# Row sums among the second heads, a projection one row tile later, and a scaling between two exponentials: three reorderings in a graph-attention and diffusion kernel

## The chip, the cores and the metric

The kernel runs on one NeuronCore of a Trainium2 chip. Its engines work side by side, each through its own queue of instructions: PE (TensorE, matrix products and transposes into the PSUM memory), DVE (VectorE), ACT (ScalarE), POOL (GpSimd), and SP (SyncE), which here only starts DMA transfers. The metric is the device time of one execution in microseconds (us), the median of several runs; lower is better.

## What is computed

N = 2708 nodes with 512 features, a dense adjacency `adj` of zeros and ones. Two layers follow one another. Both begin with a layer norm and a relu and add their result to their input. The first is graph attention with 8 heads of 64 features:

```python
feats  = einsum('nf,hfd->hnd', X, W)
dense  = e_self[:, :, None] + e_neigh[:, None, :]
dense  = where(dense >= 0, dense, 0.2 * dense) + NEG_INF * (1 - A)
out    = einsum('hnm,hmd->hnd', softmax(dense), feats) + b
```

The second diffuses features over two graphs, the given one and one that it builds itself from queries and keys, by keeping the most probable nine tenths of a softmax:

```python
S  = adj + eye(n)
Rf = S / S.sum(axis=1, keepdims=True)      # row sums
Rb = S / S.sum(axis=0)[:, None]            # column sums
for s in range(2):
    A  = nucleus(softmax(Xa @ W1 @ W2 @ (Xa @ W3).T), 0.9)
    Xf, Xb, Xa = Rf @ Xf, Rb @ Xb, A @ Xa
    Z += Xf @ U1[s] + Xb @ U2[s] + Xa @ U3[s]
```

A last layer norm of X + Z closes it. The sums of the rows of `adj` are used in the second layer, and in the first one for nodes that have no neighbour at all.

## The kernel before

The nodes are 22 row tiles (`NT`) of 128 rows, the last one of 20.

**Layer 0, the heads (L434-L499).** The columns are cut into four chunks of six row tiles (the last of four). For a chunk, `adj_t` is loaded for all 22 row tiles (`a_f`, L449), converted by ACT to `a_c` (L451), and stored with the unit matrix added as `s_d` (L456) for the second layer. Then come two groups of four heads, in the text the first heads and the second heads (`gi` = 0 and 1). For each row tile `t` DVE makes four tiles `e` of attention weights (L474), one a head, and PE multiplies each with the features into six accumulators `po` (L480). After the 22nd row tile ACT copies `po` to `o_t` (L487), and the next heads can start to fill them.

`row_sums(t)` (L337-L349) sums a row tile of `adj`: twice, a DMA on SP loads half of it into the one buffer `arow` (L345), ACT passes over it with a running sum (L346); then POOL makes three tiny results (L347-L349). In the program, the row sums of a chunk's own tiles stand right behind the chunk's loads, ahead of its heads.

The tiles of a finished chunk are completed during the first heads of the next chunk, by stages that `finished(t, ...)` returns (L359-L432). `later[slot]` holds the stages that run behind row tile `slot` (0 to 21 are the first heads, 22 to 43 the second), and a chunk's tile `i` puts its stages at

```python
later.setdefault(n if final else 3 * i + n + n // 4, []).append(stage)
```

so that a tile begins every three row tiles. The stages are `turned` (six transposes of `o_t` into the two PSUM tiles `pn0` and `pn1`, L372), `shared` (division by the softmax sums), `normed` (residual and layer norm, L401), `cleared` (ACT makes `v`, L416) and `asked`. This last one transposes `v` into `pn0` (L423), has ACT copy it to `v_t` (L425), splits `v` in two halves for later products (L426), and calls `project` (L171-L189): four products of `v_t` into `pn1` (L176), two ACT copies of it (L181, L182), three POOL operations (L186-L188) and a store of keys and queries to `kq_d` (L189). Of `pn0` and `pn1` there is one buffer each. Tiles of the last chunk are finished behind the loop and leave their projection to layer 1.

The heads do not stand under `manual_schedule`: for each engine the framework itself orders the instructions that are ready, and the order of the program is a preference between them. In layer 1, `manual_schedule` keeps PE, ACT, DVE and SP in the program's order.

**Layer 1, the start of step 0 (L1314-L1446).** The rows are taken in pairs (`G` = 2). For each pair, PE makes logits, DVE their maxima, ACT the exponentials: `exp()` returns steps, first two passes per tile, `root` and `full` (L601, L608), then `points` on POOL, then passes that count (`look`, L601). Beside it, PE multiplies `s_d` with the features (`part`, L1011-L1106), a list of steps called `others`; the last step of the second part is `scaled`, in which ACT scales the four PSUM results into `yo` (L1069); the next part needs these PSUM tiles. `late()`, called once with g = -1, runs

```python
paced(fills, 2 * G)
paced(others, 1)
others.extend(part(half, 2))
paced(others, NT // 2)
paced(fills, 2 + 3 * G * NA // 2)
```

where `paced(steps, n)` runs the first n steps: here `fills` are the steps of `exp()` of the second pair and `others` holds only `scaled`.

Of the kernel before, what the change touches and what calls it, by code (L numbers as in the profile page):

```python
# [54 lines left out]
def kernel(  # L55
# [26 lines left out]
    NT = -(-N // P)  # L82
# [9 lines left out]
    G = 2  # L92
# [78 lines left out]
    def project(pool, pk, v_t, t, s, bufs=None):  # L171


        pr = rows[t]
        for k in range(KD):
            nc.tensor.matmul(pk[:, :pr], lhsT=kw[:, k, :], rhs=v_t[:, k, :pr], start=(k == 0), stop=(k == KD - 1))  # L176
        big = pool.tile([P, P], F32, name="kq_b", bufs=bufs)
        hl = pool.tile([P, 2, P], F32, name="kq_hl", bufs=bufs)
        if pr < P:
            nc.gpsimd.memset(hl, 0.0)  # L180
        nc.scalar.copy(hl[:, 1, :pr], pk[:, :pr])  # L181
        nc.scalar.mul(big[:, :pr], pk[:, :pr], 4097.0)  # L182


        high, x = hl[:, 0, :pr], hl[:, 1, :pr]
        nc.gpsimd.tensor_tensor(high, big[:, :pr], x, op=OP.subtract)  # L186
        nc.gpsimd.tensor_tensor(high, big[:, :pr], high, op=OP.subtract)
        nc.gpsimd.tensor_tensor(x, x, high, op=OP.subtract)  # L188
        nc.gpsimd.dma_start(out=kq_d[s][:, :, t * P:(t + 1) * P], in_=hl)  # L189

    def split_rows(pool, eng, x, t, to):

        pr = rows[t]
        hl = pool.tile([P, 2, D], F32, name="split_hl")
        if pr < P:
            nc.gpsimd.memset(hl, 0.0)
        nc.vector.tensor_scalar(hl[:pr, 0].bitcast(I32), x.bitcast(I32), -4096, None, op0=OP.bitwise_and)
        eng.tensor_tensor(hl[:pr, 1], x, hl[:pr, 0], op=OP.subtract)
        nc.gpsimd.dma_start(out=to[t * P:(t + 1) * P], in_=hl)
# [19 lines left out]
    with ExitStack() as l0:  # L219
# [113 lines left out]
        halves = l0.enter_context(tc.tile_pool(name="l0halves", bufs=1))  # L333
# [25 lines left out]
        def finished(t, o_t, c0, bank, final):  # L359


            pr = rows[t]
            pns, held = [], []

            def turned():
                xt = work.tile([P, D], F32, name="xt0", bufs=4)
                nc.sync.dma_start(out=xt[:pr], in_=x[cols[t], :])
                held.append(xt)
                for g in range(NG):
                    pns.append(bank(g))  # L370
                    for k in range(len(beside)):
                        nc.tensor.transpose(pns[g][:pr, k * P:(k + 1) * P], o_t[:, g, k, c0:c0 + pr], ident)  # L372

            def shared():
                den = small.tile([P, H], F32, name="den")
                rden = small.tile([P, H], F32, name="rden")
                o = work.tile([P, D], F32, name="o", bufs=4)
                held.append(o)
                o3 = o.rearrange("p (h d) -> p h d", h=H)

                def halves(x, n):
                    return x[:, :2 * n].rearrange("p (i d) -> p i d", i=2)

                def turns(g):
                    return pns[g][:pr, :3 * P].rearrange("p (i d) -> p i d", i=2)

                for g in range(NG):
                    nc.vector.tensor_scalar(halves(den[:pr, g * HG:], 2), turns(g)[:, :, P::P // HG],
                                            lone_n[:pr, t:t + 1], None, op0=OP.add)
                nc.vector.reciprocal(rden[:pr], den[:pr])  # L390
                for g in range(NG):
                    c = slice(g * HG * DH, (g + 1) * HG * DH)
                    nc.vector.scalar_tensor_tensor(halves(o[:pr, c], 2 * DH), halves(fsum[:pr, c], 2 * DH),
                                                   lone[:pr, t:t + 1], turns(g)[:, :, :P], op0=OP.mult, op1=OP.add)
                eng = nc.vector if final else nc.gpsimd
                eng.tensor_mul(o3[:pr], o3[:pr], rden[:pr].unsqueeze(2).to_broadcast([pr, H, DH]))
                eng.tensor_add(o[:pr], o[:pr], b_b[:pr])

            def normed():
                xt, o = held  # L400
                nc.vector.scalar_tensor_tensor(o[:pr], o[:pr], 0.0, xt[:pr], op0=OP.max, op1=OP.add)  # L401
                held.extend(moments(small, o[:pr], pr))
                with_beta(o)

            def with_beta(o):
                xt = held[0]
                nc.gpsimd.tensor_add(xt[:pr], o[:pr], beta_b[:pr])
                nc.gpsimd.dma_start(out=xb_d[cols[t], :], in_=xt[:pr])

            def cleared():  # L410
                _, o, mean, rs = held
                v = turn.tile([P, D], F32, name="v")
                held.append(v)
                shift = small.tile([P, 1], F32, name="shift")
                nc.vector.scalar_tensor_tensor(shift[:pr], mean, -1.0, rs, op0=OP.mult, op1=OP.mult)
                nc.scalar.activation(v[:pr], o[:pr], AF.Relu, scale=rs, bias=shift[:pr])  # L416
                nc.gpsimd.dma_start(out=va_d[cols[t], :], in_=v[:pr])

            def asked():
                v = held[4]  # L420
                pt = bank(0).rearrange("p (k d) -> p k d", k=KD)
                for k in range(KD):
                    nc.tensor.transpose(pt[:, k, :pr], v[:pr, k * P:(k + 1) * P], ident[:pr, :pr])  # L423
                v_t = work.tile([P, KD, P], F32, name="v_t", bufs=2)
                nc.scalar.copy(v_t[:, :, :pr], pt[:, :, :pr])  # L425
                split_rows(halves, nc.gpsimd, v[:pr], t, vhl_d)  # L426
                project(halves, bank(1), v_t, t, 0, bufs=2)

            def rest():
                unasked.append((t, held[4]))  # L430

            return [turned, shared, normed, cleared, rest if final else asked]  # L432

        later = {}  # L434
        unasked = []
        for ci, tiles in enumerate(tchunks):
# [4 lines left out]
            for t in range(NT):  # L441
# [12 lines left out]
                    d = slice(t * P - n0, t * P - n0 + pr)  # L454
                    nc.gpsimd.tensor_tensor(a_f[:pr, d], a_f[:pr, d], ident[:pr, :pr], op=OP.add)
                nc.sync.dma_start(out=s_d[t * P:(t + 1) * P, n0:n0 + wide], in_=a_f[:, :wide])  # L456
            for t in tiles:
                row_sums(t)
            r_bs += [shares(grp, n0, cw) for grp in hgroups[1:]]
            o_t = work.tile([P, NG, len(beside), WC], F32, name="o_t", bufs=1)  # L460
            halfs = -(-cw // 512)
# [3 lines left out]
            for gi, (grp, r_b) in enumerate(zip(hgroups, r_bs)):  # L465
                po = [[ps_o.tile([P, 512], F32, name="po") for _ in parts] for _ in beside]
                for t in range(NT):
                    pr = rows[t]
                    es = []
                    for k, slots in enumerate(beside):  # L470
                        while len(es) <= max(i for i, _ in slots):
                            i = len(es)
# [16 lines left out]
            final = ci == len(tchunks) - 1  # L489
            for i, t in enumerate(tiles):  # L490
                if final and i < 3:
                    bank = lambda g: ps_o.tile([P, 512], F32, name="po")
# [486 lines left out]
    for s in range(STEPS):  # L979
        last = s == STEPS - 1  # L980
        with ExitStack() as st:
# [136 lines left out]
            def paced(steps, n):  # L1118
                for step in steps[:n]:
                    step()  # L1120
                del steps[:n]
# [171 lines left out]
            with tc.manual_schedule(engines={PE, ACT, DVE, SP}):  # L1293
# [52 lines left out]
                for g in range(-1, NP):  # L1346
# [48 lines left out]
                    def late(g=g):  # L1395
                        if g >= 0:
                            out_ = rest_of(att)
                            if last:
                                done.extend(zip(pairs[g], out_))
                            else:  # L1400
                                mixed(pairs[g], out_, others, fills, final)
                            keeps = 0
                            while last and keeps < len(others) and others[-1 - keeps].price == 0:
                                keeps += 1
                            while len(others) > keeps or fills:
                                if last:
                                    advanced(others, min(2, len(others) - keeps))
                                else:
                                    paced(others, 2)
                                paced(fills, 1)  # L1410
                            left.extend(others)
                            others.clear()
                            for t, y in done:
                                while t not in whole:
                                    paced(left, 1)
                                settled(t, y)
                            return


                        if last:  # L1420
                            paced(fills, len(fills))
                        else:
                            paced(fills, 2 * G)
                            paced(others, 1)
                            others.extend(part(half, 2))
                            paced(others, NT // 2)
                            paced(fills, 2 + 3 * G * NA // 2)
                            looks.extend(fills)
                        if last:
                            paced(others, len(others))  # L1430
# [51 lines left out]
```

## Time and profile before

| | us |
|---|---|
| median of 3 runs (lowest, highest) | 3473.28 (3465.6, 3474.12) |
| the profiled execution | 3485.01 |
| its span, first to last instruction | 3483.2 |
| layer 0, the heads | 139 to 943 |
| row sums, first and last load | 182.5 and 474.7 |
| ACT's waits for their loads | 165.8 in 42 waits |
| projections of finished tiles (L176) | 379.8 to 893.1, 18 tiles |
| start of step 0, the scaling `yo` | 1067.6 to 1070.0 |
| mean granted clock of PE | 0.964 |

A row of the timeline has the start, the length, engine, line, operation, output and inputs, and in brackets how long the engine stood idle before and what ended that. `x48` joins that many records; an fp32 product is two records on PE. A row of the waits has the waiting and the releasing instruction, the sum, the number and the longest wait in us. A row of the windows has the stretch, its length, each engine's busy time (with records), the clock granted to PE as a share of full speed, the share of the DMA engines that is busy, and GB/s.

### The profile page before, as it was taken

What the parts mean: (1) busy time and instruction counts of PE and PEld (TensorE: products, weight loads), DVE (VectorE), ACT (ScalarE), POOL (GpSimd) and SP (SyncE); (2) the same over time, 40 slices, a digit from 0 to 9 for tenths busy, and PEclk for the clock granted to TensorE, in tenths of its full rate; (3) what the DMA queues carried; (4) which work ended last, traced back from release to release, by engine and by line L of the source; (5) the groups of instructions that cost most, each with busy time, mean ns of one, the idle gap of its engine ahead of it and who ended that gap; (6) DMA issues with size and microseconds to landing.
All of it is one profiled execution on the core that took longest, in us unless ns stands there. A gap on an engine that the chain in (4) does not pass through costs nothing. (4 is left out here: it accounts for less than half of the span.)

```text
span 3483.2 us, 44354 instructions
## 1 busy us (share of the span) xinstructions
PE 3205.4 (92%) x16033; PEld 1707.6 (49%) x16033; DVE 2582.7 (74%) x4485; ACT 1501.5 (43%) x2219; POOL 923.6 (27%) x1091
## 2 busy tenths in 40 slices
PE   8988899899988999999999999899989999988898
PEld 4542333333455446455464643555555555555554
DVE  4577899888947655463655643887999899988984
ACT  2333231011036675564667521265644554455610
POOL 4212743605231221221222222110230232213211
PEclk9998999999999999999999998999999999999999
DMA  4478554222286336244452634766444554556453
GB/s 134 157 235 267 193 169 144 75 94 80 76 299 235 113 106 208 99 166 165 142 198 98 212 112 134 263 237 203 146 156 157 202 177 144 190 175 225 150 209 123
DMA packets 240046, 580.65 MB, mean 167 GB/s; under 512 B 32863, under 2 KB 66107, under 8 KB 239657
## 3 DMA queue, kind: packets, MB, share of 16 engines
q1 hardware_dynamic: 217721, 503.38, 43.3%
q0 software_dynamic: 22064, 74.09, 5.6%
q8 instruction: 127, 2.08, 0.2%
q14 instruction: 134, 1.10, 0.1%
HBM read 471.68 MB, written 105.68 MB: 166 GB/s over the span
## 5 line engine op out<-in xcount | busy, mean ns | idle before, releaser
L1165 PE MATMUL a<-va,at 128*128 128x512 f32 (+2 forms) x1936 | 887.8, 598 | 4.9 <-ACT at L1147 4.9
L480 PE MATMUL po<-e,fw 128*32 128x384 f32 (+3 forms) x7392 | 685.1, 507 | 58.5 <-DVE e L474 29.4
L474 DVE SCALAR_TENSOR_TENSOR e<-r_b,kk,a_c 128x768 f32<-128x768 f32 (+3 forms) x704 | 667.3, 1007 | 76.9 <-PE po L480 67.9
L601 ACT ACTIVATE junk_a<-p,nth 128x2708 uint8<-128x2708 f32 (+1 forms) x240 | 612.8, 2553 | 35.3 <-POOL nth L616 30.8
L1039 PE MATMUL q<-hl,s_r 128*128 128x512 f32 x1936 | 545.4, 430 | 66.4 <-DMA s_r<-s_d 46.0
L1165 PEld LDWEIGHTS a<-va,at 128*128 128x128 f32 (+2 forms) x1936 | 338.2, 186 | 374.6 <-issue 342.8
L1039 PEld LDWEIGHTS q<-hl,s_r 128*128 128x128 f32 x1936 | 370.1, 195 | 229.4 <-issue 68.2
L480 PEld LDWEIGHTS po<-e,fw 128*32 128x32 f32 (+1 forms) x7392 | 256.0, 112 | 451.5 <-issue 270.2
L1147 ACT COPY at<-t 128x512 f32<-128x512 f32 (+3 forms) x308 | 140.8, 478 | 647.1 <-PE t L1143 643.3
L680 DVE SCALAR_TENSOR_TENSOR junk<-p,th 128x2708 bf16<-128x2708 f32 (+1 forms) x132 | 409.5, 3102 | 3.0
L1059 PE MATMUL q<-u_k,v 128*128 128x512 f32 x704 | 318.2, 594 | 1.1 <-ACT v L1049 1.1
L1042 PE MATMUL q<-s_r,hl 128*128 128x512 f32 (+1 forms) x1056 | 283.2, 414 | 28.8 <-DMA s_r<-s_d 17.9
L1042 PEld LDWEIGHTS q<-s_r,hl 128*128 128x128 f32 x1056 | 196.8, 192 | 108.5 <-issue 54.1
L1059 PEld LDWEIGHTS q<-u_k,v 128*128 128x128 f32 x704 | 134.0, 191 | 159.8 <-issue 155.0
L569 ACT COPY p<-t 128x452 f32<-128x452 f32 (+2 forms) x264 | 130.9, 537 | 172.5 <-PE t L567 131.9
L876 DVE MAX8 vn<-keep 128x8 f32<-128x2708 f32 (+1 forms) x66 | 196.8, 2981 | 2.3
L567 PE MATMUL t<-keys,q_t 128*128 128x452 f32 x528 | 156.4, 420 | 40.1 <-ACT p L569 39.5
L594 DVE TENSOR_REDUCE nmx<-p 128x1 f32<-128x2708 f32 (+1 forms) x44 | 130.5, 2967 | 65.4 <-ACT p L569 65.4
L1212 PE MATMUL a<-u_k,v_t 128*128 128x512 f32 (+1 forms) x352 | 169.0, 619 | 5.5 <-ACT yo L1219 3.3
L155 POOL TENSOR_SCALAR ln_rs<-ln_mv 128x1 f32<-128x1 f32 x66 | 49.7, 754 | 407.9 <-DVE ln_mv L154 406.7
L1143 PEld LDWEIGHTS t<-ident,keep 128*128 128x128 f32 (+1 forms) x968 | 114.7, 139 | 77.0 <-issue 47.3
L1143 PE MATMUL t<-ident,keep 128*128 128x128 f32 (+1 forms) x968 | 145.2, 272 | 3.1 <-ACT p L569 3.0
(311 smaller groups left out, 3436.2 us busy)
## 6 DMA issues: line engine op xcount, KB each, us to landing
hl<-vhl_d SPq DMA_DIRECT2D x132, 512.0 KB
s_r<-s_d SPq DMA_DIRECT2D x264, 256.0 KB
hl<-fhl_d SPq DMA_DIRECT2D x132, 512.0 KB
hl<-bhl_d SPq DMA_DIRECT2D x132, 512.0 KB
u_k<-in_L_gnn_U_dram SPq DMA_DIRECT2D x184, 256.0 KB
arow<-in_adj_dram SPq DMA_DIRECT2D x42, 677.0 KB
s_d<-a_f SPq DMA_DIRECT2D x66, 384.0 KB
s_r<-s_d SPq DMA_DIRECT2D x132, 192.0 KB
```

Source lines behind the costliest of these rows:

```text
L474: nc.vector.scalar_tensor_tensor(es[i][:pr, :cw], r_b[:pr, i, :cw], kk[:pr, t, grp[i]:grp[i] + 1], a_c[t][:pr, :cw], op0=OP.max, op1=OP.mult)
L480: nc.tensor.matmul(po[k][n][q * w:(q + 1) * w, :b - a], lhsT=of if d < DH else of.to_broadcast([pr, w]), rhs=es[i][:pr, a:b], start=(t == ...
L567: nc.tensor.matmul(pl[:, :c1 - c0], lhsT=q[:, i], rhs=self.keys[:, c0:c1], start=(i == 0), stop=(i == 1))
L601: nc.scalar.activation(junk[:pr], self.p[i][:pr], func, **kw)
L680: nc.vector.scalar_tensor_tensor(self.junk_b[:pr], p, th, p, op0=OP.is_ge, op1=OP.mult, accum_out=dst)
L876: v.max(vs, keep[0][:pr])
L1039: nc.tensor.matmul(half[j], lhsT=s_r[:, j * P:(j + 1) * P], rhs=hl[:, h], start=(c == 0 and h == 0), stop=(c == NT - 1 and h == 1))
L1042: nc.tensor.matmul(half[j][:, :w], lhsT=hl[:, h, j * P:(j + 1) * P], rhs=s_r[:, :w], start=(c == 0 and h == 0), stop=(c == NT - 1 and h == 1))
L1059: nc.tensor.matmul(half[j], lhsT=across_t[-1][k][:, j * P:(j + 1) * P], rhs=u_k, start=(start and k == 0), stop=(start and k == KD - 1))
L1143: nc.tensor.transpose(pt[:rows[c], j, :pr], keep[i][:pr, cols[c]], ident[:pr, :pr])
L1165: nc.tensor.matmul(pa[:pr], lhsT=at[:rows[c], j, :pr], rhs=va[:rows[c], c, :], start=(c == 0), stop=(c == NT - 1))
L1212: nc.tensor.matmul(pz[i][:rows[t]], lhsT=v_t[i][:, k, :rows[t]], rhs=u_k, start=(k == 0), stop=(k == KD - 1))
```

## The change

There are three edits, in layer 0's heads and at the start of layer 1. No operation is added or removed.

1. The row sums of a chunk's tiles are no longer called ahead of its heads. They become entries of `later` at slots 22, 25, 28, 31, 34 and 37, in the chunk's second heads.
2. `asked` is cut in two. The transposes, the copy to `v_t` and the split stay in it; the projection becomes a sixth stage `answered`, whose slot is by the formula above one row tile later.
3. In `late()` of step 0, the scaling `yo` is called between the exponentials of the first and of the second tile of the pair.

```diff
                 nc.scalar.copy(v_t[:, :, :pr], pt[:, :, :pr])
+                held.append(v_t)
                 split_rows(halves, nc.gpsimd, v[:pr], t, vhl_d)
-                project(halves, bank(1), v_t, t, 0, bufs=2)
+
+            def answered():
+                project(halves, bank(1), held[5], t, 0, bufs=2)
...
-            return [turned, shared, normed, cleared, rest if final else asked]
+            return [turned, shared, normed, cleared] + ([rest] if final else [asked, answered])
...
-            for t in tiles:
-                row_sums(t)
+            for i, t in enumerate(tiles):
+                later.setdefault(NT + 3 * i, []).append(lambda t=t: row_sums(t))
...
-                            paced(fills, 2 * G)
+                            paced(fills, G)
                             paced(others, 1)
+                            paced(fills, G)
                             others.extend(part(half, 2))
```

## The prediction

> **What bounds the kernel now.** I read the page first, then PE's waits, the windows by stage, the tile views, the timeline around the three places the change names. PE is the busiest engine:
>
> ```profile
> PE 3205.4 (92%) x16033; PEld 1707.6 (49%) x16033; DVE 2582.7 (74%) x4485; ACT 1501.5 (43%) x2219; POOL 923.6 (27%) x1091
> ```
>
> So what counts is time in which PE stands still. The chain of what ended last reaches back only to 2779 us and says nothing of the changed stages, so I take PE's waits (line, releaser, us in total, times, longest):
>
> ```profile
> PE po L480 <- DVE e L474: 29.4, 43, 5.4
> PE po L480 <- ACT o_t L487: 28.5, 3, 14.7
> PE pn L176 <- ACT v_t L425: 18.5, 7, 3.0
> PE q L1042 <- ACT yo L1069: 8.6, 1, 8.6
> ```
>
> Each of the last three belongs to one edit. Layer 0's heads run from 139 to 943 us. By PE's accumulations its stages are 139-240 and 240-345 (chunk 1, first and second heads), 345-476, 476-569 (chunk 2), 569-699, 699-793 (chunk 3), then chunk 4. The two in which tiles are finished while row tiles run (columns: PE, PEld, DVE, ACT, POOL busy, clock, DMA):
>
> ```profile
> 345.00:476.00 131.00, 116.63 (x1142) 47.69 (x1138) 114.35 (x146) 40.38 (x69) 95.88 (x105) 0.92 0.55 188
> 569.00:699.00 130.00, 112.23 (x1098) 45.28 (x1091) 113.97 (x144) 9.46 (x21) 76.04 (x74) 0.93 0.22 80
> ```
>
> PE and DVE are equally full here: whichever is freed, the other is late next.
>
> **Part 1, row sums to the second heads: 0 us.** The edit removes and adds no instruction: 44 loads (0.33 us of SP each), 44 ACT passes (1.33 us + 0.19), 66 small POOL ones. What they cost now is head-of-line waiting: ACT waits 166 us for their loads and works strictly in its queue's order. At 240 us the copies of `po` stand behind such a wait:
>
> ```profile
> 238.27 1.33 ACT L346 ACTIVATE arow<-arow 128x1354 f32<-128x1354 f32 x1 [4.52 <-DMA arow<-in_adj_dram]
> 239.60 1.98 ACT L487 COPY o_t<-po 128x384 f32<-128x384 f32 x5
> 240.12 7.24 PE L480 MATMUL po<-e,fw 128*32 128x384 f32 x56 [13.22 <-ACT o_t L487]
> ```
>
> 13.22 us there, 14.72 at 343.64. After them the granted clock is 0.74 (240-250) and 0.76 (344-352), which costs another 10 x 0.26 + 8.4 x 0.24 = 4.6. So 32.5 us would be the prize. But does the edit move the row sums? This stage is not under a hand-written order, and the trace shows that the place in the program doesn't decide:
>
> ```profile
> L345 SPq DMA_DIRECT2D arow<-in_adj_dram x44: 302/328/807, 182.5 to 474.7; - x44
> L449 SPq DMA_DIRECT2D a_f<-in_adj_t_dram x88: 303/333/1617, 133.6 to 769.8; - x88
> ```
>
> Row sums of chunks 3 and 4 stand behind those chunks' `a_f` loads in the program, yet all 44 are issued by 475 us, one each 6.8 us ((474.7 - 182.5) / 43), while chunk 3's own loads mostly come after 479. What holds a row sum is its one buffer. Nothing that it needs changes, so a later place in the program should leave it where it is: right behind chunk 1's `a_f` loads, ahead of the copies at 240. Bounds: -32.5 if it does move; above, +14.7, if the copies at 476 or 569, free now, come to stand behind a row sum as those at 344 do. Beside the finishing itself row sums cost little: 131.0 us with 20 passes in the stage, 130.0 with none. I take 0, by the row of `arow`.
>
> **Part 2, the projection a row tile later: -12.0 us.** Eight matmul records per tile (1.16 us), two ACT copies (L181, L182: 0.27 each), three POOL operations (L186-L188: 0.63 + 0.75 + 0.71) and the store (0.73 of POOL's queue) move, for 18 tiles. The keys that need the stores are loaded from 956 us; the last store moves from about 896 to 901 (L181 for the last such tile is at 893.5 now, a row tile there lasts 5 us). POOL is busy 76 of 130 us and no engine waits for these. Now:
>
> ```profile
> 644.69 0.81 ACT L416 ACTIVATE v<-o,shift,ln_rs 128x512 f32<-128x512 f32 x1 [17.24 <-DVE shift L415]
> 645.41 0.56 ACT L425 COPY v_t<-pn 128x512 f32<-128x512 f32 x1
> 646.02 1.16 PE L176 MATMUL pn<-v_t,kw 128*128 128x128 f32 x8 [3.02 <-ACT v_t L425]
> 647.22 0.27 ACT L181 COPY kq_hl<-pn 128x128 f32<-128x128 f32 x1 [1.25 <-PE pn L176]
> 647.38 0.28 ACT L182 ACTIVATE kq_b<-pn 128x128 f32<-128x128 f32 x1
> 650.47 0.87 PE L372 MATMUL pn<-ident,o_t 128*128 128x128 f32 x6
> ```
>
> ACT serves the next tile's `v` first, which waits for its layer norm; `v_t` is late and PE stands 3.02 us. A row tile is 48 records of 83 ns (96 in 7.95 us), 4.0 us: more than 3.02, so the wait goes, six times 3.02-3.03 and once 0.32.
>
> The clock has to be weighed. After a 3.03 us gap the windows show it lowered:
>
> ```profile
> 624.90:627.00 2.10, 2.10 (x12) 1.88 (x16) 1.74 (x3) 0.00 (x0) 0.39 (x1) 0.50 0.37 142
> 627.00:632.20 5.20, 5.20 (x38) 1.52 (x38) 2.23 (x2) 0.45 (x2) 3.77 (x6) 0.62 0.20 80
> 646.00:650.40 4.40, 4.38 (x46) 2.15 (x46) 3.50 (x4) 0.45 (x2) 3.00 (x5) 1.00 0.20 69
> ```
>
> The Trainium skill ("TensorE: Matmul & The Clock Gate", section "HAM oscillation — how this bites in real kernels") lets gaps up to about 3.4 us pass without a lower clock. By it the seven gaps cost 18.5 us and no more. By the rows five of six gaps lose (1 - clock) x window too: 2.4, 1.7, 3.0, 1.7, 1.7 = 10.5, so 29.0 us of PE in all. The row decides.
>
> How much reaches the end is set by DVE, late next. Its waits for PE are 23.3 us in 345-476 and 12.4 in 569-699; 18.2 and 3.3 of these lie at the stages' starts and have another cause. That leaves 5.1 + 9.1 = 14.2 us, about half (0.49) of PE's 29.0. (By the skill's rule: 18.5 x 0.49 = 9.1.)
>
> Against it stands a new wait. `turned` of the tile after next falls to the same row tile and writes the same single `pn1` that the projection writes; it must wait for L181 and L182. Queued behind it on PE are the next row tile's products, for which DVE then waits. Before, a row tile lay between. Twelve tiles have such a follower (tiles 1 to 4 of six, in three chunks). The copies end 0.5 us after the projection when ACT is free (647.18 to 647.66), which transposes into `pn0` and some products cover. In chunk 2 ACT is in a row sum's wait 55% of the time (72.5 / 131), half of a wait is 2 us: 4 x 0.55 x 2 x 0.49 = 2.2 us. So 14.2 - 2.2 = 12.0. Bounds: -18.5 (DVE's waits elsewhere shrink too) and +13 (below).
>
> **Part 3, scaled results between two exponentials: -2.7 us.** In step 0, once:
>
> ```profile
> 1065.06 2.55 ACT L608 ACTIVATE p<-p,nmx 128x2708 f32<-128x2708 f32 x1
> 1067.61 2.40 ACT L1069 ACTIVATE yo<-q,cinv 128x512 f32<-128x512 f32 x4
> 1068.33 7.08 PE L1042 MATMUL q<-s_r,hl 128*128 128x512 f32 x24 [8.59 <-ACT yo L1069]
> 1100.08 0.97 ACT L569 COPY p<-t 128x452 f32<-128x452 f32 x2 [2.63 <-PE t L567]
> ```
>
> PE's last product before was done at 1059.73. ACT is idle from 1057.8 to 1062.1, waiting for the second tile's maximum: four scalings (2.4 us) fit, so the second exponential isn't delayed. PE starts at about 1060.6, 7.7 us earlier. But its next results, L567, are copied by ACT only after nine passes that end at 1097.4, and these hang on the second exponential. The copies move from 1100.08 to 1097.4: 2.7 us, and PE, late from there on, carries it to the end. The other 5 us become PE's wait for L569. Bounds: 0 and -7.7.
>
> **The sum.** 0 - 12.0 - 2.7 = -14.7 us against the profiled execution's 3485.0 (span 3483.2 and 1.8 around it): 3470.3. The runs' median, 3473.3, is 11.7 lower, so 3473.3 - 14.7 = 3459.
>
> **Rivals.** (a) *Row sums really move.* Then the waits at 240 and 344 go, 32.5 us more, and DVE (16.0 and 18.2 us idle there) follows: 3427. Against it: the row of `arow`. (b) *Slower: the wait on `pn1`.* If ACT is tied up at all 12 followers, by row sums or by `v` in another order, each costs what `v_t` costs now, 3.0 us and 1.5 of clock: 12 x 4.5 x 0.49 = 26.6, less 14.7: +12, 3485. It decides from 14.7 / (12 x 0.49) = 2.5 us per follower. For it: ACT's queue is strict; against: in chunks 3 and 4 ACT is idle nine tenths. (c) *The edits do nothing:* the ordering puts the projection where it was, because it picks what is ready: only part 3, 3471.
>
> **Chances.** Forecast 53% (own range 3450-3466), (a) 16%, (c) and like results 12%, (b) and other losses of a reshuffled order 19%. A measurement of this kernel tells about 0.3%, 10.4 us, from no change. Faster: 0.82 of the forecast and all of (a), 0.60; same: the rest of the forecast and (c), 0.21; slower: 0.19. The range takes in (a) and (b) and leaves out only a worse order: 3427 to 3487.
>
> **What would show it.** Right: no PE wait on `v_t` in 345-700 and clock 1.00 there; waits on `o_t` unchanged at 13-15 us; the wait on `yo` under 1 us and one on L569 in its place. Wrong: first `arow` load well after 240; PE waiting at L372 for ACT kq; DVE's waits for PE unchanged although PE's are gone.

## The result, and the profile after

The changed kernel takes 3463.96 us (median of 7 runs, 3460.43 to 3469.56) against 3473.57 us before (7 runs beside them): a ratio of 0.9966, 95% interval 0.9952 to 0.998, or 11.8 us less (6.9 to 16.7); the two medians lie 9.6 apart. The forecast was 14.3 below the first median, 14.7 below the profiled execution. The profiled execution after took 3462.71 us, with a span of 3460.9.

PE's waits after, and a row of DVE's waits after and before (lines of the heads stand three further down than before: L483 was L480, L490 was L487):

```profile
PE po L483 <- DVE e L477: 38.7, 41, 5.6
PE po L483 <- ACT o_t L490: 26.1, 3, 13.3
...
PE pn L372 <- ACT kq_b L182: 4.0, 2, 3.4
...
PE pn L176 <- ACT v_t L425: 0.5, 1, 0.5
```

```profile
DVE o L401 <- POOL o L397: 20.3, 8, 3.8
```

```profile
DVE o L401 <- POOL o L397: 2.6, 1, 2.6
```

PE's 18.5 us on `v_t` are gone but for 0.5, and its row on `yo` too. The 26.1 us on `o_t` stay. New are 4.0 us on `kq_b`, 9.3 more on `e`, and, on DVE, 17.7 more on `o` from POOL. This last one no step of the prediction had.

The stages, from the first copy into `o_t` of one to that of the next, in us. "Part 2 alone" and "part 1 alone" are runs told below; the queues of the latter are those of the kernel before, so its column is a second execution of them:

| stage | before | part 1 alone | part 2 alone | all three |
|---|---|---|---|---|
| chunk 1, second heads | 103.5 | 101.2 | 101.4 | 102.1 |
| chunk 2, first heads | 131.8 | 131.6 | 131.2 | 130.5 |
| chunk 2, second | 88.8 | 88.7 | 88.1 | 89.8 |
| chunk 3, first heads | 138.4 | 138.4 | 127.4 | 126.7 |
| chunk 3, second | 90.5 | 90.5 | 89.8 | 88.2 |
| chunk 4, first heads | 101.7 | 101.7 | 97.6 | 97.6 |
| chunk 4, second | 47.9 | 47.9 | 49.0 | 49.0 |

Two executions of the same queues agree within 0.3 us in six stages of seven here. A third, part 3 alone, whose heads have the old order too, agrees within 0.6 us in the three first heads, but its second heads of chunks 1 and 3 are up to 3 us shorter (100.3 and 87.1): differences of that size in these two stages say nothing. The gain is 11 us in chunk 3's first heads and 4 in chunk 4's; chunk 2's, where ACT also serves row sums, gained next to nothing. The windows of chunks 2 and 3, first heads, after:

```profile
341.00:471.40 130.40, 114.59 (x1120) 45.95 (x1124) 106.97 (x141) 38.97 (x67) 93.14 (x104) 0.94 0.57 189
561.00:687.80 126.80, 115.42 (x1164) 46.26 (x1156) 114.00 (x148) 13.07 (x29) 78.65 (x74) 0.96 0.25 89
```

Chunk 3's and chunk 4's first heads before, and chunk 4's after:

```profile
564.00:702.00 138.00, 120.23 (x1170) 48.46 (x1166) 120.58 (x150) 13.10 (x30) 76.17 (x75) 0.93 0.25 87
792.60:894.30 101.70, 90.28 (x666) 30.99 (x662) 91.60 (x150) 13.93 (x31) 64.98 (x75) 0.97 0.26 90
```

```profile
776.00:873.60 97.60, 85.39 (x658) 29.09 (x652) 91.67 (x148) 13.51 (x29) 65.89 (x74) 1.00 0.25 89
```

Chunk 3 adds up: PE waits 11.6 less on `v_t` and 5.1 more on `e`, and is busy 4.8 less with nearly as many records, at a granted clock of 0.96 against 0.93: 11.3 of the 11.7. Chunk 4 had no wait on `v_t`; there PE is busy 4.9 us less, at 1.00 against 0.97.

A lower clock comes in stretches. Before, there was one of 6.8 us near the start of each of the two stages (566.1 and 794.8), although PE ran there without a wait; after, there is none. What chunk 3 has left after are three of 3.4 us (596.4, 634.0, 671.5), each within 0.3 us of the end of a wait for `e` of 1.1 to 1.4 us. The stretch at 566.1 before; the one at 634.0 after, with PE's row:

```profile
566.10:572.90 6.80, 6.80 (x48) 1.91 (x44) 3.46 (x5) 1.05 (x3) 0.00 (x0) 0.50 0.85 270
```

```profile
634.00:637.40 3.40, 3.40 (x24) 1.11 (x24) 2.92 (x5) 0.99 (x2) 2.09 (x2) 0.50 0.27 87
633.87 5.76 PE L483 MATMUL po<-e,fw 128*32 128x384 f32 x44 [1.10 <-DVE e L477]
```

### The profile page after: what moved, and what is told of

The parts are those of the page before. It is cut to its first block, busy times and chain, and to the rows that moved or that the text cites. A ratio compares the mean times of both kernels' runs of the same rounds, so it can differ in the third digit from the quotient of the medians.

```text
span 3460.9 us, 44356 instructions
## 1 busy us (share of the span) xinstructions
PE 3183.6 (92%) x16033; PEld 1695.6 (49%) x16033; DVE 2573.5 (74%) x4485; ACT 1502.3 (43%) x2219; POOL 933.6 (27%) x1091
## 5 line engine op out<-in xcount | busy, mean ns | idle before, releaser
L483 PE MATMUL po<-e,fw 128*32 128x384 f32 (+3 forms) x7392 | 675.7, 502 | 65.7 <-DVE e L477 38.7
L477 DVE SCALAR_TENSOR_TENSOR e<-r_b,kk,a_c 128x768 f32<-128x768 f32 (+3 forms) x704 | 659.7, 997 | 50.4 <-PE po L483 41.8
L483 PEld LDWEIGHTS po<-e,fw 128*32 128x32 f32 (+1 forms) x7392 | 256.9, 112 | 449.7 <-issue 260.0
L1045 PE MATMUL q<-s_r,hl 128*128 128x512 f32 (+1 forms) x1056 | 279.7, 409 | 17.7 <-DMA s_r<-s_d 15.1
L572 ACT COPY p<-t 128x452 f32<-128x452 f32 (+2 forms) x264 | 131.5, 537 | 172.0 <-PE t L570 128.0
L597 DVE TENSOR_REDUCE nmx<-p 128x1 f32<-128x2708 f32 (+1 forms) x44 | 130.5, 2967 | 63.9 <-ACT p L572 63.9
```

Of the source, the lines that this page charges most:

```text
L477: nc.vector.scalar_tensor_tensor(es[i][:pr, :cw], r_b[:pr, i, :cw], kk[:pr, t, grp[i]:grp[i] + 1], a_c[t][:pr, :cw], op0=OP.max, op1=OP.mult)
L483: nc.tensor.matmul(po[k][n][q * w:(q + 1) * w, :b - a], lhsT=of if d < DH else of.to_broadcast([pr, w]), rhs=es[i][:pr, a:b], start=(t == ...
L1045: nc.tensor.matmul(half[j][:, :w], lhsT=hl[:, h, j * P:(j + 1) * P], rhs=s_r[:, :w], start=(c == 0 and h == 0), stop=(c == NT - 1 and h == 1))
```

## The experiments

The theory at this point: part 2 carries the gain, part 1 moves nothing, part 3 is small, and DVE's new wait for POOL eats some of part 2. The ratios are to the kernel before, from the runs beside each, with 95% intervals; the changed kernel stands at 0.9966.

**Each part alone.** Kernels with one of the three edits of the diff above and nothing else.

> Part 1 alone. Theory: the place in the program doesn't set the place in the queues, so nothing changes: ratio to the kernel before 1.000 within 0.002, PE's waits on o_t stay at 28 us within 2 (13 and 15), arow loads from about 182 to 475 us. Since nothing moves, its trace is also a second look at the kernel before, whose profiled execution lay 11.7 us over its median: I expect a span near 3472 and not 3483. Rival (row sums move): about 3441, ratio 0.991, both waits gone.

Measured: 0.9998 (0.9985 to 1.001). Instruction by instruction all five queues came out in the order of the kernel before (two records of DVE in layer 1 that start 4 ns apart aside). The edit is no edit, and waits on `o_t` are 25.3 us. The span of the same queues was 3476.8 where the one before had 3483.2: single executions lie 6 us apart.

> Part 2 alone. Theory: it carries nearly all of the gain of the changed kernel: ratio 0.9966 to 0.9985 (5 to 12 us), the last o_t copy about 17 us earlier than 943.5 by the trace, PE's wait on v_t at 0 to 1 us, and DVE's new wait for POOL at L401 about 20 us. Rival 1 (the gain comes from part 3): ratio 1.000. Rival 2 (all three edits are needed together): ratio over 0.9985 and layer 0 ends less than 10 us earlier.

Measured: 0.9969 (0.9953 to 0.9984), the whole gain. The last `o_t` copy starts at 925.7 against 941.0 and 943.5, DVE's wait at L401 is 18.1 us, PE's on `kq_b` 4.6.

> Part 3 alone. Theory: PE starts step 0's first products 7 to 8 us earlier, its wait of 8.3 us on yo goes, and 5 us of it come back as a wait for the copies of t, since these follow nine looks; 2.7 us remain: ratio 0.9992, which the runs can hardly tell from 1.000. In the trace the time from the last o_t copy to the first copy of step 0's t shrinks by 2.7 us. Rival 1 (PE's start decides): that time shrinks by 7 to 8 us, ratio 0.998. Rival 2 (all hidden): not at all, 1.000.

Measured: 1.0008 (0.9994 to 1.0021). ACT's and PE's timeline of this kernel, and the same place in the trace of part 1 alone, which has the old order:

```profile
1047.97 2.40 ACT L1069 ACTIVATE yo<-q,cinv 128x512 f32<-128x512 f32 x4
1087.63 0.95 ACT L569 COPY p<-t 128x452 f32<-128x452 f32 x2
1088.19 7.53 PE L567 MATMUL t<-keys,q_t 128*128 128x452 f32 x20 [11.09 <-ACT p L569]
```

```profile
1064.64 2.40 ACT L1069 ACTIVATE yo<-q,cinv 128x512 f32<-128x512 f32 x4
1065.36 7.38 PE L1042 MATMUL q<-s_r,hl 128*128 128x512 f32 x24 [8.32 <-ACT yo L1069]
1098.39 0.97 ACT L569 COPY p<-t 128x452 f32<-128x452 f32 x2 [3.92 <-PE t L567]
```

Counted from ACT's scaling of `xe` just before (1032.48 and 1040.77), the first copy of `t` comes 55.15 us later instead of 57.62: 2.5 us, the mechanism as forecast. PE's 8.3 us have become 11.1. Fourteen copies on, at the next pass that counts, 1.4 of the 2.5 us are left. The rest is clock: the products behind the wait of 11.1 us began at 0.50, those of the other trace ran at 1.00.

```profile
1088.19:1091.85 3.66, 3.66 (x9) 2.33 (x9) 2.24 (x4) 2.00 (x5) 0.00 (x0) 0.50 0.24 97
```

```profile
1098.39:1105.30 6.91, 5.93 (x22) 2.98 (x20) 1.45 (x3) 5.25 (x11) 1.06 (x2) 1.00 0.93 355
```

The runs show no gain, but their interval reaches to 2.1 us of it, so they cannot rule out the 1.4.

**Row sums that really move.** What is missing is a dependency, so this kernel makes one: the scale of the summing pass is a 1.0 that ACT computes from an `e` of the second heads.

```diff
-        def row_sums(t):
+        def row_sums(t, e):
+            one = small.tile([P, 1], F32, name="one")
+            nc.scalar.activation(one, e[:, :1], AF.Copy, scale=0.0, bias=1.0)
...
-                nc.scalar.activation(arow, arow, AF.Copy, accum_out=half[:pr, i:i + 1])
+                nc.scalar.activation(arow, arow, AF.Relu, scale=one[:pr], accum_out=half[:pr, i:i + 1])
...
-                later.setdefault(NT + 3 * i, []).append(lambda t=t: row_sums(t))
+                later.setdefault(NT + 3 * i + 2, []).append(lambda t=t: row_sums(t, es[0]))
```

> The changed kernel, with each tile's two row-sum passes made to depend on an e of the second heads (a scale of 1.0 that ACT makes from it), so that they really move. Theory (the copies of po stand behind row sums): PE's 26 us on o_t go, and 4 to 5 us of lower clock with them: 20 to 32 us less than the changed kernel, ratio to the kernel before 0.987 to 0.991. Rival: the stage is limited by its loads (DMA share 0.8), and the copies then stand behind an a_c pass or DVE takes over: under 8 us, ratio over 0.994. Other rival: the row sums now stall the second heads, where PE had none of this: ratio 0.997 to 1.003.

Measured: 0.9906 (0.9884 to 0.9928), about 21 us below the changed kernel. The loads of the changed kernel and of this one (tile view), and the copies at the end of chunk 1's second heads (timeline):

```profile
L345 SPq DMA_DIRECT2D arow<-in_adj_dram x44: 301/328/1367, 182.9 to 473.9; - x44
```

```profile
L347 SPq DMA_DIRECT2D arow<-in_adj_dram x44: 301/328/692, 184.0 to 889.1; - x44
```

```profile
340.87 1.22 ACT L490 COPY o_t<-po 128x384 f32<-128x384 f32 x3
345.42 1.22 ACT L490 COPY o_t<-po 128x384 f32<-128x384 f32 x3
```

```profile
314.12 2.30 ACT L492 COPY o_t<-po 128x384 f32<-128x384 f32 x6
```

Now all six copies run in one go, 26.7 us earlier; with a row sum between them they came in two halves. PE has no wait on `o_t` left. Chunk 1's first heads gave 14.5 us, its second 12.2, chunk 2's first 3.9. Taken back were 2.5 us in chunk 2's second heads and 3.6 in chunk 4's, where row sums now fall, and 2.7 in chunk 4's first heads, where none falls (chunk 4's first pass is at 855.5, after them): there PE is busy 3.1 us more at a clock of 0.97, against 1.00 in the changed kernel.

A variant sums the last chunk's four tiles in that chunk's first heads, whose row tiles last twice as long:

```diff
+                at = 5 * i + 2 if ci == len(tchunks) - 1 else NT + 3 * i + 2
-                later.setdefault(NT + 3 * i + 2, []).append(lambda t=t: row_sums(t, es[0]))
+                later.setdefault(at, []).append(lambda t=t: row_sums(t, es[0]))
```

> The gated row sums of before (made to wait for an e through a 1.0 from ACT; projection one row tile later), only that the last chunk's four tiles are summed in that chunk's first heads, whose row tiles last twice as long. Theory: the gated kernel gave back 2.7 us in chunk 4's first and 3.6 us in its second heads, where DVE's e waits for ACT's 1.0 that stands behind a row sum's load; the second of these goes: chunk 4's second heads 52.6 to 49, ratio 0.9906 to 0.9895. Rival: the first heads, which also finish chunk 3's tiles, lose as much as the second gain: 0.990 to 0.992, first heads over 103 us.

Measured: 0.988 (0.9855 to 0.9905), chunk 4's second heads 49.5 us instead of 52.6. That stage moved as forecast; the intervals of the two whole kernels overlap.

**POOL's queue.** First, `normed` and `cleared` one row tile later, so that POOL has longer for `o`:

```diff
-                    later.setdefault(n if final else 3 * i + n + n // 4, []).append(stage)
+                    later.setdefault(n if final else 3 * i + n + (n > 1), []).append(stage)
```

> The changed kernel, with normed and cleared of each tile one row tile later, so that POOL has a row tile more for o before DVE adds to it. Theory (the later projection put POOL's work for kq ahead of o in POOL's queue, and DVE's wait for it eats part of the gain): DVE's wait at L401 falls from 20.3 to under 5 us, PE's wait for e by about 9, and the kernel is 5 to 10 us faster than the changed one: ratio to the kernel before 0.994 to 0.995. Rival (DVE has slack there): no difference to the changed kernel, 0.9966. Other rival: v comes too late for its transposes, PE waits on v in their place: 0.998 to 1.002.

Measured: 0.9975 (0.9962 to 0.9987), no better than the changed kernel. DVE's wait at L401 did fall, to 3.4 us, and chunk 3's first heads to 123.2. But PE's waits:

```profile
PE pn L372 <- ACT kq_b L182: 19.7, 8, 3.9
...
PE pn L423 <- ACT v L416: 9.4, 5, 2.3
```

ACT's `v` of the next tile now stands ahead of the copies of `kq`, and chunk 4's first heads rose to 102.5. This is the prediction's slower rival in part: 19.7 us of waits on `pn1`, eight times, where it had 12 times 3.0 us, and 9.4 on `v`. By the ratios about three quarters of the gain are left.

Then the projection two row tiles later than before, by itself and with the gated row sums:

```diff
-                    later.setdefault(n if final else 3 * i + n + n // 4, []).append(stage)
+                    later.setdefault(n if final else 3 * i + n + n // 4 + n // 5, []).append(stage)
```

> The changed kernel with the projection two row tiles later than before instead of one, in a row tile in which no turned and no new o falls. Theory (what is left of part 2's gain is eaten by two new queues: PE's transposes behind kq's copies, 4 to 5 us, and o behind kq's work on POOL, 20 us of DVE waits, which cost PE about 9): both go, ratio to the kernel before 0.992 to 0.995, 5 to 13 us less than the changed kernel; chunk 2's first heads shrink from 130.5 to about 126. Rival (DVE's wait has slack, as moving the norm suggested): 0.996 to 0.997. Other rival: the transposes of turned now hold pn1 for DVE's reads, and the projection waits there with all products behind it: 0.998 or more.

> Both: gated row sums (20.8 us less than the changed kernel by themselves) and the projection two row tiles later. Theory: the two are in different stages except chunk 2's first heads, so they add: ratio 0.9906 minus 0.0015 to 0.004: 0.987 to 0.989. In chunk 2's first heads, where no row sum is left in ACT's queue, less is to be had than with row sums there. Rival: with row sums gone ACT is free and the two-later projection brings nothing: 0.9906.

Measured: 1.0013 (0.9999 to 1.0026), and 0.9906 (0.9882 to 0.9929). Both theories fell; the second ratio is the one that its rival named. PE's wait on `kq_b` is gone, DVE's for `o` 2.3 us; but DVE's `shift`, which needs POOL's `ln_rs`, waits 29.1 instead of 16.3 us, and PE 53.5 us on `e`. In POOL's queue the three operations on `kq` now stand among those for the layer norm. Each of the three places tried has its own wait of DVE for POOL, or of PE for ACT.

A third kernel leaves POOL's three operations on `kq` out in layer 0 (the keys stay unsplit):

```diff
+        if bufs:
+            nc.scalar.copy(hl[:, 0, :pr], pk[:, :pr])
+            nc.scalar.mul(hl[:, 1, :pr], pk[:, :pr], 0.0)
+            nc.gpsimd.dma_start(out=kq_d[s][:, :, t * P:(t + 1) * P], in_=hl)
+            return
```

> The changed kernel with POOL's three operations on the projected keys of layer 0 left out (the keys go into the rest of the kernel unsplit; ACT still copies twice, and the store stays), so only layer 0's stages are to be read. Theory (kq's 2 us of POOL per tile stand ahead of o and cost DVE 20 us of waits, PE 9): DVE's wait at L401 falls under 5 us; chunk 2's first heads go from 130.5 to 126 to 128, chunk 3's from 126.7 to 121 to 123. Rival (DVE's waits there are slack, and the 134 us of two row tiles later had another cause): both stages within 1 us of the changed kernel's.

Measured in the stages: 130.0, 125.0 and 95.4 us in the first heads of chunks 2, 3 and 4, so 0.5, 1.7 and 2.2 less. (The whole kernel's ratio, 0.9893, says nothing here: layer 1 works with other keys.) DVE's wait for `o`, L401 elsewhere:

```profile
DVE o L406 <- POOL o L402: 15.8, 7, 4.3
```

The theory fell again: without a single operation on `kq`, 15.8 of the 20.3 us remain. In two of the eight waits the split of `v` stands between POOL's two operations on `o`. POOL's timeline of the changed kernel at one of them, with DVE's answer:

```profile
607.50 1.19 POOL L396 TENSOR_TENSOR o<-o,rden 128x512 f32<-128x512 f32 x1
608.65 2.00 POOL L198 TENSOR_TENSOR split_hl<-v,split_hl 128x512 f32<-128x512 f32 x1
610.61 1.28 POOL L397 TENSOR_TENSOR o<-o,b_b 128x512 f32<-128x512 f32 x1
...
611.91 0.69 DVE L401 SCALAR_TENSOR_TENSOR o<-o,xt 128x512 f32<-128x512 f32 x1 [2.41 <-POOL o L397]
```

Before, the same operation came right behind the projection, ahead of both on `o` (L198 at 609.5, L396 at 613.0, L397 at 614.8).

But in four of the eight waits, 9.2 us, POOL had nothing to do ahead of `o`: it stood idle until DVE's `rden` came. What changed there is DVE's own queue. The same tile before (the addition of L401 follows at 638.54, without a wait) and after:

```profile
633.98 4.64 DVE L474 SCALAR_TENSOR_TENSOR e<-r_b,kk,a_c 128x768 f32<-128x768 f32 x3
634.15 1.70 POOL L396 TENSOR_TENSOR o<-o,rden 128x512 f32<-128x512 f32 x1 [2.76 <-DVE rden L390]
635.93 1.88 POOL L397 TENSOR_TENSOR o<-o,b_b 128x512 f32<-128x512 f32 x1
```

```profile
627.01 0.96 DVE L477 SCALAR_TENSOR_TENSOR e<-r_b,kk,a_c 128x768 f32<-128x768 f32 x1
627.17 1.70 POOL L396 TENSOR_TENSOR o<-o,rden 128x512 f32<-128x512 f32 x1 [0.54 <-DVE rden L390]
628.95 1.27 POOL L397 TENSOR_TENSOR o<-o,b_b 128x512 f32<-128x512 f32 x1
630.25 0.69 DVE L401 SCALAR_TENSOR_TENSOR o<-o,xt 128x512 f32<-128x512 f32 x1 [2.29 <-POOL o L397]
```

Between `rden` and the addition DVE had three `e` in all twelve tiles of chunks 2 and 3. In the changed kernel the framework left one or two in eight of the twelve, and these are the eight waits. In the other four of them (11.1 us) row sums, `kq` or the split stand in POOL's queue as well. The other kernels fit: with the projection two row tiles later there are three `e` again in every tile (2.3 us of waits), with `normed` later four or more (3.4 us).

The next kernel takes the split off POOL:

```diff
-                split_rows(halves, nc.gpsimd, v[:pr], t, vhl_d)
+                split_rows(halves, nc.vector, v[:pr], t, vhl_d)
```

> The changed kernel with the split of v (L198) on DVE instead of POOL in layer 0: POOL gets 18 times 1.7 to 2.0 us less between the two operations on o, DVE 18 times 0.7 us more (12 us). Theory (POOL's queue is what holds DVE at L401): those 20 us fall under 6, DVE has 2 to 6 us less in all, ratio 0.995 to 0.9965, so equal to the changed kernel within the interval, with its waits moved. Rival (DVE's waits are slack): DVE gets 12 us more work in the two stages where it is late next, ratio 0.998 to 1.000.

Measured: 0.9928 (0.9906 to 0.9949), a larger gain than either theory gave, though DVE has 18 operations of 0.75 us more. The first heads of chunks 2 to 4 last 128.0, 120.3 and 91.1 us. DVE's waits at L401 are 10.1. The rest is in the groups of DVE in chunk 4's first heads (mean ns behind the busy time), the changed kernel and then this one, each above the same operation in its second heads:

```profile
L477 DVE SCALAR_TENSOR_TENSOR e<-r_b,kk,a_c 128x404 f32<-128x404 f32 x84 | 72.7, 912 | 0.7 <-PE po L483 0.6
...
L477 DVE SCALAR_TENSOR_TENSOR e<-r_b,kk,a_c 128x404 f32<-128x404 f32 x84 | 46.9, 635 | 0.0
```

```profile
L477 DVE SCALAR_TENSOR_TENSOR e<-r_b,kk,a_c 128x404 f32<-128x404 f32 x85 | 65.3, 818 | 0.7 <-PE po L483 0.6
...
L477 DVE SCALAR_TENSOR_TENSOR e<-r_b,kk,a_c 128x404 f32<-128x404 f32 x84 | 46.4, 634 | 1.8 <-PE po L483 1.8
```

An `e` takes longer where POOL works beside it. By the same view of the three stages' first and second heads the excess is (1197 - 1023) x 77 + (1185 - 1017) x 84 + (912 - 635) x 84 ns = 51 us of DVE in the changed kernel and 31 here: the 20 us less pay for the 13.5 more. With the 10.2 us less of waits at L401 that makes some 17 us of DVE; the three stages are 15.4 us shorter.

**Spreading the gated row sums otherwise.** The gate's 1.0 made by DVE, six, eight, eight and no tiles in the four chunks' second heads (every second row tile in chunks 2 and 3), with the projection two row tiles later:

```diff
-            nc.scalar.activation(one, e[:, :1], AF.Copy, scale=0.0, bias=1.0)
+            nc.vector.tensor_scalar(one, e[:, :1], 0.0, 1.0, op0=OP.mult, op1=OP.add)
...
-            for i, t in enumerate(tiles):
-                later.setdefault(NT + 3 * i + 2, []).append(lambda t=t: row_sums(t, es[0]))
+            n = -(-(NT - len(tchunks[0])) // 2)
+            mine = [list(range(TC)), list(range(TC, TC + n)), list(range(TC + n, NT)), []][ci]
+            for i, t in enumerate(mine):
+                later.setdefault(NT + (2 if ci else 3) * i + 2, []).append(lambda t=t: row_sums(t, es[0]))
```

> As the run before, but the gate's 1.0 is made by DVE instead of ACT (so no e is held by an ACT queue that stands at a load), and chunk 4's four tiles are summed in the second heads of chunks 2 and 3 (6, 8, 8, 0 tiles). Theory: gated row sums gave back 2.7 and 3.6 us in chunk 4's first and second heads and 2 to 4 in chunk 2's second; most of this goes: 4 to 8 us less than the run before, ratio 0.985 to 0.987. Rival: eight tiles in 90 us are too many for one buffer, and copies of po at the ends of chunks 2 and 3 stand behind row sums again: waits on o_t over 5 us, ratio over 0.988.

Measured: 0.9992 (0.9973 to 1.001). The rival had it: waits on `o_t` of 16.7 us are back, 15.0 of them at the end of chunk 2's second heads, where a row sum's pass stands between the two halves of the copies, as in the changed kernel, and that stage lasts 107 us instead of 89. Whether the density or the gate on DVE did it was not tried apart.

**The two that gained, together.** The variant of 0.988 with the split on DVE:

> Both versions that were faster than the changed kernel in one: gated row sums with the last chunk's in its first heads (ratio 0.988), and the split of v on DVE (0.9928 by itself, 0.9966 without). Theory (the first frees ACT's queue ahead of the copies of po at 240 and 344 us, the second POOL's and DVE's in the first heads of chunks 2 to 4; they are different waits): they add, 0.988 x 0.9928 / 0.9966 = 0.9842, within 0.982 to 0.987, and the three first heads last 123, 119 to 121 and 91 to 94 us. Rival (what DVE is freed of was already slack once row sums are gone): 0.987 to 0.989.

Measured: 0.983 (0.9802 to 0.9858), 3411.78 us (3410.74 to 3421.24) against 3473.91. The two gains add, and the kernel is some 47 us faster than the changed one (0.9966 - 0.983 of 3473). PE has no wait on `o_t` any more, 0.8 us on `kq_b` and none on the heads' `v_t`; what the heads still wait for is `e`:

```profile
PE po L486 <- DVE e L480: 39.2, 47, 5.4
```

## Why the prediction was right, and where its steps were not

- **Part 1, 0 us: right, for the reason given.** The same queues came out, and the loads still run from 182.9 to 473.9. The prize of 32.5 us was about right in its place: gating brought 30.6 us in the three stages named, of which 21 reached the end.
- **Part 2, -12.0 us: right in the sum** (part 2 alone: 10.8, interval 5.6 to 16.3), **wrong in how it is spread, so in part by luck.** The step gave chunk 2 5.1 and chunk 3 9.1 before the new wait; the stages gave 0.4, 10.9, and 4.1 in chunk 4, for which nothing was forecast. In chunk 2, PE's 6.4 us on `v_t` went, and 4.0 on `kq_b` and 3.6 on `e` came. In chunk 4 the gain is a higher clock, which the step had nowhere.
- **The clock: the row was the better guide to what it does, but not to what it is worth.** Stretches at 0.50 did stand behind waits of 3.0 us, and after the change behind shorter ones: by the rule that the prediction weighed there would be none. That is also why the clock did not reach 1.00 in chunk 3, as forecast, but 0.96: new waits for `e` lower it in their turn. Of the 10.2 us less of such stretches in chunk 3, 3.4 are at the old waits on `v_t`; 6.8 are the one at the stage's start, whose 3.3 us of DVE's waits the prediction had set aside as another cause. What brings that one is not shown: the gated kernel, with the moved projection, has both stretches again (5.9 and 6.8 us), and its chunk 3 took 127.5 us all the same, its chunk 4 100.3.
- **The new wait on `pn1`, 2.2 us of the end:** the mechanism as described, 4.0 us of PE's waits in two stretches, both in chunk 2. The slower rival didn't come because ACT was free, and does come in part where its queue is reordered.
- **"No engine waits for these" (POOL): this step failed.** It was read off the trace of before, and DVE waits 17.7 us more at L401. The prediction named POOL's busy share, and took for granted that the other queues would keep their order. They did not: DVE's addition came to stand one or two `e` behind the `rden` that releases POOL, instead of three, and POOL's two operations on `o` alone last 3.0 us; in half of the waits, work on `kq`, row sums or the split of `v` delays them further.
- **Part 3, -2.7 us: right in place (2.5 us at the first copies), but not carried to the end**: PE's wait for L569 became 11.1 us and not 5, the clock behind it fell to 0.50, which this step did not count though part 2's did, and 1.4 us were left. The runs show no gain (1.0008).
- **Left open:** the last copy into `o_t` starts at 923.9 and 925.7 us in the traces of the changed kernel and of part 2 alone, and between 933.8 (part 3 alone) and 943.5 in the three with the old heads, so 8 to 20 us earlier; the first heads of chunks 2 to 4 alone are 15.5 to 17.3 shorter. The runs say 11 to 12, their interval reaches to 16.7. From the last copies into `o_t` to the end it is 2538 us after and 2537 to 2541 before, so nothing is given back there; single executions of one program lie 6 us apart.

## What to carry to other kernels

Where a framework orders ready instructions, a later place in the program moves nothing by itself; a dependency does, and what the move is worth is then read from the wait of the engine behind the queue's head. When an operation is moved, compare each in-order queue of the new program with the old one, also of engines from which nothing was moved: here POOL was busy 62% of chunk 3's stage, and DVE still waited for it, because its own next step had come closer to its request. An operation on a less busy engine can cost the busy one more than doing it itself.

## What the runs showed of the hardware

DVE and POOL hold each other up. An `e` of 128x404 takes 0.63 us in stages with hardly any POOL work and 1.65 us beside one POOL operation of 1.67 us (timeline of the changed kernel):

```profile
798.98 1.67 POOL L198 TENSOR_TENSOR split_hl<-v,split_hl 128x512 f32<-128x512 f32 x1 [1.40 <-DVE split_hl L197]
799.43 1.65 DVE L477 SCALAR_TENSOR_TENSOR e<-r_b,kk,a_c 128x404 f32<-128x404 f32 x1
```

The `e` ends just behind POOL's operation. That it is POOL, and not the transfers or PE's products of these stages, shows in the whole timeline: of the 254 `e` in the first heads of chunks 2 to 4, the 50 with no POOL operation beside them took at most 1.02 us (0.64 in chunk 4), and each of the 85 longer ones has one beside it. POOL is held up too: its addition to `o` (L397) takes 1.27 us where DVE stands waiting for it, and 1.88 beside `e` (rows of the tile before and after, above).

The Trainium skill ("SBUF — State Buffer", section "SBUF: two separate sides") says why this can be: DVE with two SBUF inputs and a GpSimd operation that reads SBUF share one port pair under an exclusive lock. The rows agree, though they show the delay and not the lock; the prediction had not counted it, and it is 51 us of DVE in three stages.
